# Three small moves in a tuned encoder-decoder kernel: the query weights' sums, a read-out's engine, one block's first token sums

## The chip, the cores and the metric

The kernel runs on one core of a Trainium2 chip. The metric is the device time of one execution in microseconds (us); the median of the runs counts. Five engines work side by side, each through its own queue in order: TensorE (PE in the profile, its weight loads PEld), VectorE (DVE), ScalarE (ACT), GpSimd (POOL) and SyncE (SP), which issues the DMA transfers. They meet by semaphores.

## The reference, cut to what matters

One encoder layer over a short context (2 x 77 rows) and one decoder layer over 2 x 2048 rows, all in float32, width 512, 16 heads of 32, feed-forward width 2048.

```python
memory = encoder_layer(ctx_1024)                     # attention, then relu feed-forward, 77 rows a batch
y = x                                                # (2, 2048, 512)
yn = ln(y, dec_n1)
y = y + mha(yn, yn, dec_sa_in_w, dec_sa_out_w, bias=relative + causal)
y = y + mha(ln(y, dec_n2), memory, dec_ca_in_w, dec_ca_out_w, bias=relative)
y = y + relu(ln(y, dec_n3) @ ff1_w.T + ff1_b) @ ff2_w.T + ff2_b
# inside mha: q = xq @ wq.T + bq; the scores are divided by sqrt(32), the softmax runs over keys
```

## The kernel before, in words

The 2 x 2048 rows are cut into eight blocks (b, m) of 512 rows, numbered x = 0 to 7. For causal self-attention a block has 4 groups g of 4 heads and 4 tiles t of 128 rows, so 16 units a block; unit n has a slot n. The order is written by hand. `light[n]` holds steps run at the start of a slot, `jobs[n]` the projections on TensorE, `late[n]` steps at its end; between slots stand scores (L375, read out by VectorE in L384 and L391, with the negated row maxima at L401), exponentials on ScalarE (L406), transposes on TensorE (L426, copied out at L431 and L433) and the products with the values (L455, copied out by ScalarE at L466 for a batch's first block). Every engine keeps the order in which the code emits.

The projections of blocks 1 to 3 of each batch use a Strassen-like scheme of seven products of quarters. It needs sums of weight quarters, made once by GpSimd and stored in DRAM, and four sums T1 to T4 of token quarters for each block (`token_sums`, L961, from the normalised and transposed rows `nT`). T1 and T2 lie in buffers `xt`, T3 and T4 in `xr`.

- The k, v and output weights' sums are made by `wc_sums` (loads L977, sums L981 and L961, stores `wc_store` L993) in slots 2, 9 and 12, those of the query weights by three steps: `q_load` (8 transfers, L1013), `q_sums` (four scalings L1020, an add L1022, three subtractions L961) and `q_store` (7 transfers, L1029, from where `pair_job` loads them at L1037). All use the same eight spare pieces of `kT`: four take the loaded quarters, four the sums.
- The encoder, a long chain of small stages, runs beside block 0: stage n goes to `late[n]`, or `late[n + 2]` from the tenth on. In slots 6 to 9 GpSimd subtracts the maxima (L617), adds a bias row to the residual (L655) and divides by the sums (L629) for it; VectorE adds the bias and takes the maxima (L615, L616, and sums at L627); ScalarE does the exponentials (L622); TensorE the scores (L606).
- In the same slots block 1's rows are loaded (L275), their statistics taken by VectorE (L282 to L285), a power and the centring done by GpSimd (L286, L293), the transposes by TensorE (L305) and their read-out by ScalarE and VectorE (L310, L312).
- `pair_job` with parts (1, 6) makes two products of a query group pair side by side in one PSUM bank (L1048). The first is read out with its bias at L1054, the second added to that at L1055, by VectorE.
- Block results get their residual on GpSimd at L1106 and L1107 (`out_done`) once the rows have been loaded; the softmax division of a group is one GpSimd product at L493.

After the self-attention of all blocks come cross attention and feed-forward (from about 1500 us on).

Of the kernel before, what the change touches and what calls it, by code (L numbers as in the profile page):

```python
# [10 lines left out]
F32 = mybir.dt.float32  # L11
AF = mybir.ActivationFunctionType
ALU = mybir.AluOpType
# [4 lines left out]
P = 128  # L18
B, T, S, D = 2, 2048, 77, 512
# [5 lines left out]
NMB = T // MB  # L25
# [29 lines left out]
def tile_encoder_decoder(ctx: ExitStack, tc: tile.TileContext, ins, out):  # L55
    nc = tc.nc
    x, src = ins["x"], ins["ctx_1024"]
# [13 lines left out]
    qbias = const.tile([P, NC], F32, name="qbias")  # L71
# [87 lines left out]
    with (  # L159
# [20 lines left out]
        def bank():  # L180

            ring.append(ring.pop(0))
            return psum[:, ring[-1], :]
# [11 lines left out]
        wbig, xs, xr, ots_at = {}, {}, {}, {}  # L195
# [214 lines left out]
        got = {}  # L410
# [547 lines left out]
        gp, ve = nc.gpsimd, nc.vector  # L958

        def minus(engine, out, a, b):  # L960
            engine.tensor_tensor(out, a, b, ALU.subtract)  # L961
# [3 lines left out]
        def sum_n(name, of):  # L965
            minus(gp, of(name), *(of(a) for a in T_OF[name]))
# [42 lines left out]
        def q_load(z):  # L1009
            src = ins["dec_sa_in_wT"][:, :D].rearrange("(c k p) (h r o) -> p c h r k o", c=2, k=2, h=2, r=2)  # L1010
            for i, (r, c) in enumerate(((0, 0), (0, 1), (1, 0), (1, 1))):
                for h in range(2):
                    nc.sync.dma_start(  # L1013
                        z[i][:, ts(h, TOK)].rearrange("p (k o) -> p k o", k=2), src[:, c, h, r]
                    )

        def q_sums(z):
            q = {(0, 0): z[0], (0, 1): z[1], (1, 0): z[2], (1, 1): z[3]}
            for t in z[:4]:
                gp.tensor_scalar(t, t, SCALE, None, ALU.mult)  # L1020
            s1, s2, s3, s4 = z[4:]
            gp.tensor_tensor(s1, q[1, 0], q[1, 1], ALU.add)  # L1022
            minus(gp, s2, s1, q[0, 0])
            minus(gp, s3, q[0, 0], q[1, 0])
            minus(gp, s4, q[0, 1], s2)

        def q_store(z):
            for i, t in enumerate((z[0], z[1], z[3], *z[4:])):
                nc.sync.dma_start(saq_d[i], t)  # L1029

        def pair_job(b, m, h, parts):

            def load():
                w = sb.tile([P, NC, P], F32, name="wqk", tag="wqk", bufs=3)
                for j, i in enumerate(parts):
                    src = saq_d[Q_OPS.index(PARTS[i][0])][:, ts(h, TOK)]
                    nc.sync.dma_start(w[:, 2 * j : 2 * j + 2, :], src.rearrange("p (k o) -> p k o", k=2))  # L1037
                return w

            def run(w):  # L1040
                if parts[0] == 1:
                    for g in (2 * h, 2 * h + 1):
                        qTs[b, m, g] = sb.tile([P, MB], F32, name="q", tag="q", bufs=3)
                mm = bank()
                for j, i in enumerate(parts):
                    n = of_nT(b, m, PARTS[i][1])
                    for c in range(2):
                        nc.tensor.matmul(mm[:, ts(j, TOK)], w[:, 2 * j + c, :], n[:, c, :], start=c == 0, stop=c == 1)  # L1048
                d = {
                    f"{r + 1}{c + 1}": qTs[b, m, 2 * h + r][:, ts(c, TOK)] for r in range(2) for c in range(2)  # L1050
                }
                got = [mm[:, ts(j, TOK)] for j in range(len(parts))]
                if parts == (1, 6):
                    nc.scalar.activation(d["11"], got[0], AF.Identity, bias=qbias[:, 2 * h : 2 * h + 1])  # L1054
                    ve.tensor_tensor(d["12"], got[1], d["11"], ALU.add)  # L1055
                elif parts == (7, 4):
                    ve.scalar_tensor_tensor(d["22"], got[0], qstep[:, h : h + 1], d["12"], ALU.add, ALU.add)
                    ve.tensor_tensor(d["21"], got[1], d["22"], ALU.add)
                elif parts == (2, 5):
                    q = qTs[b, m, 2 * h]  # L1060
                    ve.tensor_tensor(q, mm, q, ALU.add)
                    ve.tensor_tensor(d["22"], got[1], d["22"], ALU.add)
                else:
                    assert parts == (3,)
                    ve.tensor_tensor(d["12"], got[0], d["12"], ALU.add)

            return load, run, True
        n_tiles = {}
        PARTS = {
# [5 lines left out]
        def of_nT(b, m, name):  # L1075
            if name[0] == "T":
                return n_tiles[b, m][int(name[1]) - 1].rearrange("p (c o) -> p c o", c=2)
            r, c = int(name[0]) - 1, int(name[1]) - 1
            return nTs[b, m][:, 2 * r : 2 * r + 2, ts(c, TOK)]

        def token_sums(b, m):
            n_tiles[b, m] = [
                sb.tile([P, D], F32, name=tag, tag=tag, bufs=2) for tag in ("xt", "xt", "xr", "xr")
            ]
            for name in ("T1", "T2", "T3", "T4"):
                sum_n(name, lambda n: of_nT(b, m, n))

        o_tiles = {}
# [92 lines left out]
        light = {n: [] for n in range(-1, len(units) + NU)}  # L1181
        late = {n: [] for n in light}

        for x, (b, m) in enumerate(blocks):
            u = x * NU
# [12 lines left out]
            else:  # L1198
# [7 lines left out]
                for at, names in todo.items():  # L1206
                    for name in names.split():
                        h, parts = "ab".find(name[0]), tuple(int(i) for i in name[1:])
# [29 lines left out]
                    on = nc.vector if x == 1 and t % 2 else nc.scalar  # L1238
                    light[turned_at].append(lambda b=b, m=m, t=t, on=on: norm_turn(b, m, t, on=on))
            if not first:  # L1240
                (late[u - 5] if x == 1 else light[u - 5 if x == NMB + 1 else u - 6]).append(
                    lambda b=b, m=m: token_sums(b, m)
                )
            for g in range(NC):
                apart = not (x == len(blocks) - 1 and g >= NC - 2)
                d = spread(b, m, g) if apart else divide(b, m, g)
# [63 lines left out]
        )  # L1310
        spare = [kT[:, g, (2 + h) * MB : (3 + h) * MB] for g in range(NC) for h in range(2)]
        light[1].append(q_steps)
        light[5].append(lambda: q_load(spare))
        late[6].append(lambda: q_sums(spare))
        late[7].append(lambda: q_store(spare))
        for n, kind in ((2, "k"), (9, "v"), (12, "o")):
            light[n].append(lambda kind=kind: wc_sums(sa_name[kind], True, spare, sa_from[kind]))
            late[n + 1].append(lambda kind=kind: wc_store(sa_d[kind], spare))
# [141 lines left out]
        u = 2 * NU  # L1460
# [5 lines left out]
        u = 6 * NU  # L1466
# [522 lines left out]
```

## Time and profile before

| | |
|---|---|
| median of 3 runs | 2736.42 us (2736.1 to 2736.77) |
| the profiled execution | 2739.72 us, its span in the trace 2737.9 us |
| busy share of the span | PE 99%, PEld 81%, DVE 67%, ACT 56%, POOL 37% |
| POOL, 98 to 130 us | 31.44 of 32 us |
| PE, 98 to 130 us | 24.64 of 32 us, granted clock 0.84 |

The span runs from the first to the last instruction of the profiled execution. Times in a timeline are microseconds from the span's start; a row merges neighbours of one kind, and its bracket names the idle time of the engine just before it and what ended it. The granted clock is the share of TensorE's full clock in that stretch.

### The profile page before, as it was taken

To read this page: it belongs to the slowest core of one execution; us is meant where nothing else is said; L and a number is where in the kernel's file an instruction comes from. 1 tells how busy PE (TensorE), PEld (TensorE's weight loads), DVE (VectorE), ACT (ScalarE), POOL (GpSimd) and SP (SyncE) were. 2 spreads that over 40 slices of the span, in tenths; PEclk is the share of its full clock that TensorE was granted. 3 is DMA by queue.
4 is the path that set the end of the run, shared out by engine and by line. 5 is a ranking of instruction groups with operands and counts; after the bars stand their busy time and mean duration, and the time that the engine had idled before them with its cause. 6 is when DMAs were issued, how large, how long until landed. Compare 5 with 4: busy or idle time off the path is not lost.

```text
span 2737.9 us, 68226 instructions
## 1 busy us (share of the span) xinstructions
PE 2710.3 (99%) x26606; PEld 2216.0 (81%) x26606; DVE 1836.3 (67%) x5390; ACT 1540.5 (56%) x3006; POOL 1002.5 (37%) x844
## 2 busy tenths in 40 slices
PE   9899999999999999999999999999999999999998
PEld 5578877777876677777777877898989898989898
DVE  5676588888876577688788793646464746464645
ACT  3445557767787546767767785444444444444431
POOL 1702226500210512313300103465646564646456
PEclk9999999999999999999999999999999999999999
DMA  8634446511212531342411106575758575756575
GB/s 224 194 108 130 137 142 180 164 56 48 63 48 72 143 91 59 113 142 80 138 56 35 61 20 228 166 219 166 218 167 242 166 219 166 220 166 219 149 225 185
DMA packets 296276, 385.10 MB, mean 141 GB/s; under 512 B 41184, under 2 KB 165648, under 8 KB 295826
## 3 DMA queue, kind: packets, MB, share of 16 engines
q1 hardware_dynamic: 295954, 380.73, 46.1%
q8 instruction: 211, 3.46, 0.5%
q14 instruction: 111, 0.91, 0.1%
HBM read 334.15 MB, written 46.47 MB: 139 GB/s over the span
## 4 chain that ended last, share of the span: by engine, by line
PE 94%; DVE 2%; ACT 1%; POOL 1%; issue 1%; DMA 0%; SPq 0%; DVEq 0%; POOLq 0%; ACTq 0%
PE psum L426 18%; PE psum L1633 14%; PE psum L1662 12%; PE psum L375 11%; PE psum L455 9%; PE psum L1136 8%; PE psum L1796 3%; PE psum L1753 3%; PE psum L1048 2%; PE psum L865 2%; PE psum L835 1%; PE psum L873 1%; PE psum L589 1%; PE psum L239 1%; PE psum L810 1%; PE psum L226 1%
## 5 line engine op out<-in xcount | busy, mean ns | idle before, releaser
L406 ACT ACTIVATE pp<-pp,nm 128x128 f32<-128x128 f32 (+15 forms) x512 | 612.1, 1201 | 29.3 <-DVE nm L401 28.7
L384 DVE TENSOR_SCALAR_CACHE_REDUCE pp<-psum 128x512 f32<-128x512 f32 (+3 forms) x1024 | 556.2, 591 | 53.2 <-PE psum L375 50.7
L433 ACT COPY pts<-psum 128x512 f32<-128x512 f32 (+2 forms) x730 | 382.5, 580 | 309.6 <-PE psum L426 260.9
L426 PE MATMUL psum<-ident,pp 128*128 128x128 f32 x4352 | 531.3, 277 | 4.9 <-ACT nT L310 2.4
L426 PEld LDWEIGHTS psum<-ident,pp 128*128 128x128 f32 x4352 | 472.6, 141 | 57.6 <-DVE pp L384 21.7
L375 PE MATMUL psum<-kT,q 32*128 32x512 f32 (+3 forms) x2560 | 335.0, 559 | 8.1 <-ACT oT L466 4.2
L455 PEld LDWEIGHTS psum<-pts,vv 128*32 128x32 f32 x8704 | 225.6, 110 | 127.8 <-DVE pp L384 55.4
L1662 PE MATMUL psum<-pp 128*128 128x128 f32 x2560 | 304.5, 276 | 1.9 <-POOL pp L961 1.6
L431 DVE COPY pts<-psum 128x512 f32<-128x512 f32 (+3 forms) x406 | 252.5, 654 | 78.5 <-PE psum L426 76.4
L1662 PEld LDWEIGHTS psum<-pp 128*128 128x128 f32 x2560 | 296.3, 192 | 8.6 <-issue 2.8
L455 PE MATMUL psum<-pts,vv 128*32 128x128 f32 x8704 | 278.7, 275 | 0.7 <-DVE mx L391 0.3
L961 POOL TENSOR_TENSOR pp<-pp 128x512 f32<-128x512 f32 x159 | 212.8, 1355 | 112.8 <-DMA pp<-in_dec_ff_wT_dram 51.7
L1633 PE MATMUL psum<-vv,pp 128*128 128x256 f32 x1024 | 236.2, 381 | 0.0
L375 PEld LDWEIGHTS psum<-kT,q 32*128 32x128 f32 x2560 | 145.7, 183 | 111.5 <-issue 39.9
L1633 PEld LDWEIGHTS psum<-vv,pp 128*128 128x128 f32 x1024 | 190.3, 190 | 25.8 <-issue 0.5
L391 DVE CUSTOM_DVE_ANT_0 pp<-psum,bias 128x256 f32<-128x256 f32 (+1 forms) x512 | 196.0, 411 | 20.0 <-PE psum L375 19.8
L1646 DVE TENSOR_TENSOR kT<-kT,psum 128x512 f32<-128x512 f32 x96 | 65.8, 686 | 191.3 <-PE psum L1633 191.1
L1649 ACT ACTIVATE kT<-kT,vecs 128x256 f32<-128x256 f32 x192 | 87.1, 502 | 157.2 <-DVE kT L1646 156.6
L1633 PE MATMUL psum<-nT,pp 128*128 128x256 f32 x768 | 174.1, 380 | 0.0
L1633 PEld LDWEIGHTS psum<-nT,pp 128*128 128x128 f32 x768 | 144.2, 190 | 20.3 <-issue 1.6
L1670 ACT COPY oT<-psum 128x128 f32<-128x128 f32 x56 | 15.0, 268 | 238.9 <-PE psum L1662 238.9
L493 POOL TENSOR_TENSOR oT<-rirows,oT 128x512 f32<-128x512 f32 x30 | 38.4, 1281 | 290.0 <-DMA rirows<-rec 223.7
(274 smaller groups left out, 4110.7 us busy)
## 6 DMA issues: line engine op xcount, KB each, us to landing
pp<-w_d SPq DMA_DIRECT2D x520, 256.0 KB
pp<-in_dec_ff_wT_dram SPq DMA_DIRECT2D x112, 256.0 KB
bias<-tzg SPq DMA_DIRECT2D x128, 128.0 KB
pp<-wo_d SPq DMA_DIRECT2D x56, 256.0 KB
wqk<-in_dec_sa_in_wT_dram SPq DMA_DIRECT2D x52, 256.0 KB
wqk<-sa_q SPq DMA_DIRECT2D x84, 128.0 KB
vv<-in_enc_ff_wT_dram SPq DMA_DIRECT2D x8, 1024.0 KB
xr<-in_x_dram SPq DMA_DIRECT2D x32, 256.0 KB
```

The costliest lines, as they stand in the source:

```text
L375: nc.tensor.matmul(banks[r][:, : kn * P], q[rows4(r), ts(t, P)], kT[rows4(r), g, k0 * P : (k0 + kn) * P], start=True, stop=True,)
L384: nc.vector.tensor_scalar(p[:, k0 : k0 + far], s[:, :far], 1.0, None, ALU.mult, ALU.max, accum_out=st["mx"][:, r, c : c + 1],)
L391: nc.vector.tensor_tensor_reduce(p[:, k0 + far : i + 1], s[:, far:kn], near[:, 2 - (kn - far) :], 1.0, LOWEST, ALU.add, ALU.max, accum_out ...
L406: nc.scalar.activation(p, p, AF.Exp, bias=nm, accum_out=to)
L426: nc.tensor.transpose(pt[:, ts(x, P)], state[n]["p"][r][:, k], ident)
L431: nc.vector.tensor_copy(pts[:, : len(load), :], pt[:, :w])
L433: nc.scalar.copy(pts[:, : len(load), :], pt[:, :w])
L455: nc.tensor.matmul(ot[rows4(r)], vv[:, k, ts(g * HC + r, HD)], got.pop((n, k, r)), start=k == k0 and (whole or not begun), stop=k == k1 - ...
L961: engine.tensor_tensor(out, a, b, ALU.subtract)
L1136: nc.tensor.matmul(mm[:, ts(f, TOK)], left[:, c, ts(f, P)], right[:, c, :], start=c == 0, stop=c == 1,)
L1633: nc.tensor.matmul(mm[:, ts(f, TOK)], a[:, c, ts(f, P)], b[:, c, :], start=fresh and f == 0 and c == 0, stop=c == 1, skip_group_check=True,)
L1662: nc.tensor.matmul(psum[:, bank_i, ts(col, P)], lhs[:, c, :], w[:, c, :], start=fresh and k in (0, 3) and c == 0, stop=c == 3, skip_group_ ...
```

## The change

Three edits. The query weights' loads go from the start of slot 5 to the start of slot 4, their sums from the end of slot 6 to the end of slot 4, their stores from the end of slot 7 to the end of slot 6. The first product of each pair is read out by VectorE instead of ScalarE (12 places). Of the sixth block (x = 5) the sums T1 and T2 are made at the start of slot 74 instead of 75, in a function that now makes two sums a call; T3 and T4 stay.

```diff
                 if parts == (1, 6):
-                    nc.scalar.activation(d["11"], got[0], AF.Identity, bias=qbias[:, 2 * h : 2 * h + 1])
+                    ve.tensor_scalar(d["11"], got[0], qbias[:, 2 * h : 2 * h + 1], None, ALU.add)
                     ve.tensor_tensor(d["12"], got[1], d["11"], ALU.add)
...
-        def token_sums(b, m):
-            n_tiles[b, m] = [
-                sb.tile([P, D], F32, name=tag, tag=tag, bufs=2) for tag in ("xt", "xt", "xr", "xr")
-            ]
-            for name in ("T1", "T2", "T3", "T4"):
+        def token_sums(b, m, tag):
+            n_tiles.setdefault((b, m), []).extend(sb.tile([P, D], F32, name=tag, tag=tag, bufs=2) for _ in range(2))
+            for name in ("T1", "T2") if tag == "xt" else ("T3", "T4"):
                 sum_n(name, lambda n: of_nT(b, m, n))
...
-                (late[u - 5] if x == 1 else light[u - 5 if x == NMB + 1 else u - 6]).append(
-                    lambda b=b, m=m: token_sums(b, m)
-                )
+                for tag in ("xt", "xr"):
+                    (late[u - 5] if x == 1 else light[u - 5 if x == NMB + 1 and tag == "xr" else u - 6]).append(
+                        lambda b=b, m=m, tag=tag: token_sums(b, m, tag)
+                    )
...
-        light[5].append(lambda: q_load(spare))
-        late[6].append(lambda: q_sums(spare))
-        late[7].append(lambda: q_store(spare))
+        light[4].append(lambda: q_load(spare))
+        late[4].append(lambda: q_sums(spare))
+        late[6].append(lambda: q_store(spare))
```

GpSimd's queue in block 0, the difference between before (-) and after (+): L1020, L1022 and the three L961 behind them are `q_sums`; L286 and L293 are the power and the centring of block 1's first tile, L617 and L655 the encoder's.

```order
 L961 TENSOR_TENSOR kT<-kT 128x512 x3
-L286 TENSOR_TENSOR rstd<-rstd,mhalf 128x1
-L293 TENSOR_SCALAR xt<-xt,bnmv,rstd 128x512
-L617 TENSOR_TENSOR pp<-pp,emx 77x1232
-L655 TENSOR_TENSOR pp<-pp 77x512 x2
 L1020 TENSOR_SCALAR kT<-kT 128x512 x4
 L1022 TENSOR_TENSOR kT<-kT 128x512
 L961 TENSOR_TENSOR kT<-kT 128x512 x3
+L286 TENSOR_TENSOR rstd<-rstd,mhalf 128x1
+L293 TENSOR_SCALAR xt<-xt,bnmv,rstd 128x512
+L617 TENSOR_TENSOR pp<-pp,emx 77x1232
+L655 TENSOR_TENSOR pp<-pp 77x512 x2
```

The eight operations of `q_sums` now stand directly behind the key weights' sums and ahead of five operations that used to precede them.

SyncE's queue, first where the query weights' loads (L1013) now stand, and then where the stores (L1029) do: L993 stores the key weights' sums, L199 loads a slice of projection weights, L544 an encoder weight, L94 writes a bias table and L275 loads rows of block 1.

```order
 L544 DMA vv<-in_enc_out_wT_dram 128x4x512
 L993 DMA sa_k<-kT 128x512 x4
+L1013 DMA kT<-in_dec_sa_in_wT_dram 128x2x128 x8
 L199 DMA wqk<-in_dec_sa_in_wT_dram 128x4x128
 L544 DMA vv<-in_enc_ff_wT_dram 128x4x512
```

```order
 L94 DMA tz_72<-pp 16x32x384
+L1029 DMA sa_q<-kT 128x512 x7
 L275 DMA xr<-in_x_dram 128x512
 L199 DMA wqk<-in_dec_sa_in_wT_dram 128x4x128
-L1029 DMA sa_q<-kT 128x512 x7
 L275 DMA xr<-in_x_dram 128x512
```

The loads moved up past the loads and stores of one slot, and the stores past one row load and one weight load.

GpSimd's queue ahead of the sixth block, before: the last three `out_done` pairs of an earlier block, a softmax division, then the four token sums (`xt` are T1 and T2, `xr` are T3 and T4).

```order
L1107 TENSOR_TENSOR xr<-xr,wbig 128x512
L1106 TENSOR_TENSOR xr<-xr,row_dec_sa_out_b 128x512
L1107 TENSOR_TENSOR xr<-xr,wbig 128x512
L1106 TENSOR_TENSOR xr<-xr,row_dec_sa_out_b 128x512
L1107 TENSOR_TENSOR xr<-xr,wbig 128x512
L493 TENSOR_TENSOR oT<-rirows,oT 128x512
L961 TENSOR_TENSOR xt<-nT 128x512
L961 TENSOR_TENSOR xt<-nT,xt 128x512
L961 TENSOR_TENSOR xr<-nT 128x512
```

And the same place of the changed kernel, where L1104 and L1105 are the lines that were L1106 and L1107:

```order
L1105 TENSOR_TENSOR xr<-xr,wbig 128x512
L961 TENSOR_TENSOR xt<-nT 128x512
L961 TENSOR_TENSOR xt<-nT,xt 128x512
L1104 TENSOR_TENSOR xr<-xr,row_dec_sa_out_b 128x512
L1105 TENSOR_TENSOR xr<-xr,wbig 128x512
L1104 TENSOR_TENSOR xr<-xr,row_dec_sa_out_b 128x512
L1105 TENSOR_TENSOR xr<-xr,wbig 128x512
L493 TENSOR_TENSOR oT<-rirows,oT 128x512
L961 TENSOR_TENSOR xr<-nT 128x512
```

T1 and T2 went ahead of two pairs and the division.

## The prediction

> **What bounds the kernel now.** I read the page first: its busy times, then the PE's list of waits, then windows, the chain and the timelines where the waits lie.
>
> ```profile
> PE 2710.3 (99%) x26606; PEld 2216.0 (81%) x26606; DVE 1836.3 (67%) x5390; ACT 1540.5 (56%) x3006; POOL 1002.5 (37%) x844
> ...
> PE psum L375 <- ACT oT L466: 4.2, 1, 4.2
> PE psum L426 <- ACT nT L310: 2.4, 2, 2.0
> ...
> 60.00:82.00 22.00, 21.72 (x178) 11.83 (x176) 12.49 (x46) 7.98 (x26) 3.02 (x3) 1.00 0.78 213
> 82.00:98.00 16.00, 14.18 (x142) 8.13 (x142) 12.66 (x43) 7.73 (x21) 13.21 (x10) 1.00 0.70 190
> 98.00:130.00 32.00, 24.64 (x157) 17.01 (x156) 17.80 (x78) 18.26 (x54) 31.44 (x24) 0.84 0.60 190
> 130.00:200.00 70.00, 69.66 (x644) 50.87 (x643) 54.58 (x193) 30.78 (x74) 8.74 (x8) 1.00 0.40 121
> ```
>
> TensorE is busy for 2710.3 of 2737.9 us, so only its 27.6 us of idle time, and time at a lowered clock, can be won or lost quickly. The second part of the fence is the list of PE's waits (total, times, longest); the third is windows (length, then busy us of PE, PEld, DVE, ACT and POOL, granted clock, DMA share, GB/s). Between 98 and 130 us PE idles 32 - 24.64 = 7.4 us and runs at 0.84 of its clock, while POOL is busy for 31.44 of 32 us. In the window before 82 us POOL did 3.02 us of work in 22; from 130 us on PE has no gap of weight. The chain of work that ended last tells who held PE:
>
> ```profile
> 88.97 5.89 POOL kT L1020 x4
> ...
> 101.90 2.06 POOL xt L293
> 103.96 2.22 POOL pp L617
> 106.21 0.03 ACT pp L622
> ...
> 107.34 0.57 ACT oT L466
> ...
> 107.96 1.80 PE psum L375 x4
> ...
> 120.91 1.40 ACT nT L310 x4
> ...
> 122.35 1.95 PE psum L426 x12
> 124.30 2.99 PE psum L1136 x8
> ...
> 129.02 1.73 PE psum L1136 x8
> ```
>
> Read from the top: the query weights' sums hold GpSimd from 88.97 us, behind them come block 1's centring and the encoder's second subtraction L617, ScalarE's exponential L622 waits for that, the copy L466 stands behind it in ScalarE's queue, and the scores L375 on PE wait for the bank that L466 empties. This is not GpSimd's whole load but its order.
>
> **Part 1: the query weights' sums, two slots sooner.** These are GpSimd's rows and SyncE's around the old and the new place:
>
> ```profile
> 51.57 3.74 POOL L961 TENSOR_TENSOR kT<-kT 128x512 f32<-128x512 f32 x3
> 76.92 0.55 POOL L286 TENSOR_TENSOR rstd<-rstd,mhalf 128x1 f32<-128x1 f32 x1 [21.61 <-DVE rstd L285]
> ...
> 81.61 2.25 POOL L617 TENSOR_TENSOR pp<-pp,emx 77x1232 f32<-77x1232 f32 x1 [1.95 <-DVE emx L616]
> ...
> 99.97 1.27 POOL L493 TENSOR_TENSOR oT<-rirows,oT 128x512 f32<-128x512 f32 x1
> ...
> 37.71 8.23 SPq L977 DMA_DIRECT2D kT<-in_dec_sa_in_wT_dram  x4
> ...
> 55.71 0.50 SPq L199 DMA_DIRECT2D wqk<-in_dec_sa_in_wT_dram  x1
> 62.71 0.38 SPq L544 DMA_DIRECT2D vv<-in_enc_ff_wT_dram  x1
> ...
> 71.54 4.32 SPq L1013 DMA_DIRECT2D kT<-in_dec_sa_in_wT_dram  x8
> ```
>
> The eight operations took 99.97 - 88.97 = 11.0 us, the last thing behind which everything to 130 us queued. Their new place is GpSimd's idle stretch of 21.6 us from 55.3 to 76.92. SyncE has a gap there too, from 56.2 to 62.71, so the eight loads (4.32 us of issue) go out from about 55.7 to 60, perhaps 61 since earlier transfers are still in flight. How long they fly the trace of before doesn't show, as GpSimd came to them late; the nearest row is the key weights' load, last issued before 45.94, on which GpSimd worked from one operation (1.25 us) ahead of the L961 of 51.57, so from 50.3: 4.4 us from the end of issue. Taken again, the last load is there at about 65; one scaling (1.5) and four sums (5.0) follow, so GpSimd is free at 72, 5 us ahead of L286. The moved loads pass L199, L544 and the transfers between; no row in the list of PE's waits names a transfer, so a few microseconds of delay there stay hidden. The transfers behind the old place (71.54) go up to 4.3 us sooner. The stores L1029 no longer wait for late sums on SyncE, with the row load L275 of block 1's last tile behind them.
>
> What is late next. Without the 11.0 us ahead of it ScalarE's L622 runs near 95 instead of 106.21, and the 4.2 us wait of L375 is gone. But VectorE is next, and its rows say how far PE may move:
>
> ```profile
> 86.51 0.79 PE L606 MATMUL psum<-pp 32*77 32x77 f32 x32
> ...
> 87.62 0.69 DVE L282 BATCH_NORM_STATS2 bnst<-xt 128x6 f32<-128x512 f32 x1 [2.29 <-DMA xt<-in_x_dram]
> 88.64 1.62 DVE L615 TENSOR_TENSOR pp<-psum,pp 77x308 f32<-77x308 f32 x4
> ...
> 103.15 0.70 DVE L282 BATCH_NORM_STATS2 bnst<-xr 128x6 f32<-128x512 f32 x1 [2.75 <-DMA xr<-in_x_dram]
> ...
> 109.11 0.22 DVE L384 TENSOR_SCALAR_CACHE_REDUCE pp<-psum 128x128 f32<-128x128 f32 x1
> ...
> 112.29 0.42 DVE L431 COPY pts<-psum 128x256 f32<-128x256 f32 x1 [0.41 <-PE psum L426]
> 113.63 1.37 DVE L312 TENSOR_SCALAR nT<-psum,vecs 128x128 f32<-128x128 f32 x4 [0.91 <-PE psum L305]
> ...
> 102.81 0.91 PE L375 MATMUL psum<-kT,q 32*128 32x384 f32 x4
> ```
>
> From 109.11 to the L310 of 120.91 VectorE works with only two gaps, 0.41 and 0.91, both waiting for a PE on a lowered clock; at its end come that L310 and the L426 of 122.35. PE's first scores of this unit began at 102.81, so VectorE could have begun at about 103.2 (an estimate: the first head's product later) had it not waited for the load of the row of 103.15 and for the sums of the late exponentials: it can begin 109.11 - 103.2 = 5.9 us sooner. The two gaps of 1.3 us mostly close at full clock. And the wait of 2.29 us for block 1's second tile, whose load stood behind L1013, goes: L615 then starts when TensorE's L606 is done, at 86.51 + 0.79 = 87.3 instead of 88.64, 1.3 us. Together 5.9 + 1.3 + 1.3 = 8.5 us at 122.35, and after 130 us PE is bound by itself, so this carries to the end. The wait of 2 us before that L426 stays, as it is made by VectorE's and ScalarE's own work there. Bounds: at least the 4.2 us wait itself; at most all idle time and lowered clock from 82 to 130 us, 1.8 + 7.4 + 0.16 x 32 = 14.3 us. I take 8.5, the row-by-row sum.
>
> One rule on the clock: behind the 4.2 us wait the trace shows four matmuls of L375 in 1.80 us, against 0.91 for as many at 102.81, and behind the last wait of only 2 us L1136 took 2.99 us against 1.73 a little later, so 1.3 us of lowered clock stays in the sum. The Trainium skill (TensorE: Matmul & The Clock Gate, What's actually happening) puts the lowered clock after an idle window of about 3.4 us; by it the 2 us wait alone would not lower the clock and the sum would be 9.8, so the traces differ from the rule unless the earlier waits had a share.
>
> **Part 2: the read-out on VectorE.** One place shows its worth, at 1038 us; the last line is from the view of L1055, what its engine waited for in total.
>
> ```profile
> 1037.93 0.47 ACT L1054 ACTIVATE q<-psum,qbias 128x256 f32<-128x256 f32 x1
> 1038.43 0.42 DVE L1055 TENSOR_TENSOR q<-psum,q 128x256 f32<-128x256 f32 x1 [3.05 <-ACT q L1054]
> 1038.91 0.91 PE L375 MATMUL psum<-kT,q 32*128 32x384 f32 x2 [1.04 <-DVE q L1055]
> ...
>   ACT q L1054: 23.1, 11
> ```
>
> ScalarE's read-out stood behind exponentials while VectorE idled 3.05 us, and PE waited 1.04 us for the bank. On VectorE the pair runs when the products are done, within those 3.05 us: gain 1.0 us. VectorE's form of the operation isn't in the trace; its neighbour L1055 takes 0.42 for the same shape from PSUM, so 12 x 0.42 = 5.1 us more VectorE work. It is covered: VectorE idled ahead of 11 of the 12 places, 23.1 us in all, waiting for just this operation. If that cover failed everywhere the price would be the 5.1 us; I take 0.
>
> **Part 3: T1 and T2 of the sixth block.**
>
> ```profile
> 950.08 1.27 POOL L1106 TENSOR_TENSOR xr<-xr,row_dec_sa_out_b 128x512 f32<-128x512 f32 x1 [7.17 <-DMA xr<-in_x_dram]
> ...
> 956.48 1.51 POOL L961 TENSOR_TENSOR xt<-nT 128x512 f32<-128x512 f32 x1
> ...
> 959.51 1.13 PE L1048 MATMUL psum<-xt,wqk 128*128 128x256 f32 x4 [1.49 <-POOL xt L961]
> ```
>
> GpSimd idles 7.17 us ahead of 950.08 and the two sums (1.5 us each) fit in it; the two pairs behind them wait for rows that land at 950 anyway. PE's 1.49 us wait goes. T3 and T4 then follow L493 3 us sooner. Gain 1.5.
>
> **Sum.** 8.5 + 1.0 + 1.5 = 11.0 us off the profiled execution's span of 2737.9, so 2726.9. That execution took 2739.72 in all, 3.3 above the median of the runs shown, 2736.42; the difference carries over: 2725.4.
>
> **Rivals.** (a) Something else holds PE between 98 and 130 us, the norm read-outs L310 and L312 or a late transfer, and only the 4.2 us wait goes: 4.2 + 2.5 = 6.7, 2729.7. For it: VectorE's dense stretch; against: that stretch starts late for a reason that goes. (b) All idle time and lowered clock goes, 14.3 + 2.5: 2719.6. Against: the last 2 us wait is VectorE's. (c) The clock stays up behind the 2 us wait, 1.3 us more gain: 2724.1; the page on the clock named above would have it so; the row of 2.99 us speaks against. (d) Part 1 doesn't do what it says, since L622 is then held by another link (rows for L655, statistics): 2.5 us, 2733.9. (e) Slower: GpSimd works in order, and L286, L293, L617 and L655 now stand behind an operation that waits for eight loads. It costs nothing while the last load lands by 70.4 (76.92 less 6.5); L617 waited 1.95 us for VectorE, so the encoder's chain, and with it PE, feels it from 72.4 on, a microsecond each. A landing at 85 would undo part 1's gain and add 12.6: 2736.4 - 2.5 + 12.6 = 2746.5. Against: it needs 24 us of flight, where the key weights' took 4.4.
>
> **How the numbers follow.** Chances: forecast 0.54, (a) 0.16, (b) 0.08, (c) 0.10, (d) 0.08, (e) 0.04. The measurement of this kernel tells about 0.2% (5.5 us) from no change. The forecast, (b), (c) and most of (a), which sits close to the edge at 6.7, are faster by more: 0.85. (d) and 3 in 100 of (a) are the same: 0.11. (e) is slower: 0.04. The range from 2719.5 to 2730.5 reaches from (b) to just past (a) and leaves out (d), (e) and the tails.
>
> **What would show it.** In the changed profile: L1020 between 60 and 68 us and no idle PE ahead of the L375 near 102; POOL below 70% in 98 to 130; L310's wait at L426 still there near 114; no wait of PE for `xt` near 950 and none for L1055 near 1030; VectorE's L1054 at 0.42. Wrong would be an L1020 that starts after 70, an L622 for the second batch still after 100, or new waits of PE on VectorE at the twelve places.

## The result, and the profile after

Nine runs of the changed kernel took 2730.39 us in the median (2728.05 to 2733.07), nine of the kernel before 2736.77 (2735.73 to 2741.35). The medians are 6.4 us apart; the ratio on record for these runs is 0.9973, 95% interval [0.9963, 0.9983], so 7.4 us less, with 4.7 to 10.1 in the interval. The comparison was made once more on another occasion (the experiment after_again below): 0.9965 [0.9952, 0.9977], 9.6 us less. The forecast was 11.0 us less, above the first interval and inside the second, and a range of 6 to 17. The median of 2730.39 lies 0.1 us inside the slow end of that range, 2730.5. The profiled execution has a span of 2726.9 us, the span that the sum gave; it took 2728.76 in all. That the span agrees to the tenth is luck, as the steps below show: one term came out smaller, one mostly vanished, and a chance effect of the clock made up for both. The profile of before is of an execution 3.0 us above its median, and that of the changed kernel of one 1.6 us below; the prediction had carried the first of these over as a constant.

The page of the changed kernel, first part, and then two rows of PE's list of waits (total, times, longest):

```profile
PE 2707.0 (99%) x26606; PEld 2214.9 (81%) x26606; DVE 1842.0 (68%) x5402; ACT 1534.6 (56%) x2994; POOL 1000.8 (37%) x844
```

```profile
PE psum L426 <- ACT nT L310: 3.2, 2, 1.8
...
PE psum L426 <- DVE kT L1147: 0.3, 1, 0.3
```

The 4.2 us wait for L466's bank is out of the list. L310's row stayed and grew from 2.4 to 3.2. The windows view (length, busy us of PE, PEld, DVE, ACT and POOL, clock, DMA share, GB/s) of the changed kernel, the last row for the same 32 us as before:

```profile
60.00:82.00 22.00, 21.43 (x175) 11.33 (x173) 13.31 (x52) 8.05 (x26) 14.70 (x11) 1.00 0.97 251
82.00:98.00 16.00, 14.52 (x142) 8.17 (x143) 13.88 (x50) 9.50 (x25) 13.67 (x10) 1.00 0.84 235
...
98.00:130.00 32.00, 28.78 (x287) 21.27 (x285) 23.61 (x93) 18.92 (x60) 21.82 (x17) 1.00 0.64 201
```

GpSimd took 11.7 us of work forward into the 22 us where it had idled (14.70 busy instead of 3.02), and from 98 to 130 us it is busy for 21.82 instead of 31.44. PE is busy 4.1 us longer in that stretch and at the full clock, which was 0.84. The timeline of GpSimd shows the step itself:

```profile
61.27 5.88 POOL L1020 TENSOR_SCALAR kT<-kT 128x512 f32<-128x512 f32 x4 [7.01 <-DMA kT<-in_dec_sa_in_wT_dram]
67.23 1.26 POOL L1022 TENSOR_TENSOR kT<-kT 128x512 f32<-128x512 f32 x1
68.58 3.71 POOL L961 TENSOR_TENSOR kT<-kT 128x512 f32<-128x512 f32 x3
76.11 0.57 POOL L286 TENSOR_TENSOR rstd<-rstd,mhalf 128x1 f32<-128x1 f32 x1 [3.82 <-DVE rstd L285]
...
89.70 2.25 POOL L617 TENSOR_TENSOR pp<-pp,emx 77x1232 f32<-77x1232 f32 x1 [0.27 <-DVE emx L616]
```

The sums wait 7.01 us for their loads, begin at 61.27 and end at 72.3; GpSimd then idles 3.82 us ahead of L286. The second subtraction L617 runs at 89.70 instead of 103.96, when its input is there, not when the queue lets it. ScalarE and VectorE, in their timelines, follow:

```profile
92.30 1.21 ACT L622 ACTIVATE pp<-pp 77x1232 f32<-77x1232 f32 x1
95.69 0.58 ACT L466 COPY oT<-psum 128x512 f32<-128x512 f32 x1 [2.18 <-PE psum L455]
```

```profile
101.64 0.29 DVE L384 TENSOR_SCALAR_CACHE_REDUCE pp<-psum 128x128 f32<-128x128 f32 x1 [0.73 <-PE psum L375]
```

L466 now waits for PE, where PE waited for it, and VectorE's first maxima begin at 101.64 instead of 109.11. PE's timeline over the same place:

```profile
100.70 0.93 PE L375 MATMUL psum<-kT,q 32*128 32x384 f32 x8
...
108.13 1.20 PE L426 MATMUL psum<-ident,pp 128*128 128x128 f32 x9 [1.41 <-ACT nT L310]
...
113.83 1.53 PE L426 MATMUL psum<-ident,pp 128*128 128x128 f32 x12 [1.81 <-ACT nT L310]
115.19 1.89 PE L1134 MATMUL psum<-nT,wqk 128*128 128x256 f32 x8
```

Two waits for the norm's read-out are left, and behind the second one the clock stays up: the product of eight took 2.99 us before (there it was L1136) and takes 1.89.

The two programs issue the same 26606 matmuls in the same order, so the start of any one of them can be compared across traces. This table gives, for every kernel run, the start minus that of the same matmul in the trace of before; 113.83 - 122.35 is the -8.52 of its first row. The first column lies ahead of every edit: it differs by up to 1.4 us from the trace of before, and is taken off where a term is read. A term is the difference of two columns. The columns 122.35 and 131.79 of e2 and e3 lie ahead of the edits of these two kernels, so they show how far executions of the same instructions differ there: 0.75 and 3.09 us, with the first column taken off.

| at, us of before | 13.54 | 122.35 | 131.79 | 956.57 | 959.51 | 968.01 | 1036.52 | 1038.91 |
|---|---|---|---|---|---|---|---|---|
| after | -0.80 | -8.52 | -10.21 | -10.20 | -11.85 | -10.18 | -10.68 | -11.91 |
| after_again | -0.80 | -8.36 | -10.04 | -10.02 | -11.67 | -10.59 | -9.60 | -10.83 |
| after_third | -1.23 | -8.96 | -10.64 | -10.63 | -12.28 | -11.04 | -10.04 | -11.27 |
| e1_query_sums | -0.54 | -8.20 | -8.21 | -8.19 | -8.80 | -8.73 | -8.51 | -8.51 |
| e2_readout | -0.33 | -1.08 | -1.09 | -1.08 | -1.61 | -1.02 | -0.99 | -2.22 |
| e3_token_sums | 0.39 | -2.70 | -2.71 | -2.70 | -4.35 | -3.95 | -4.61 | -4.61 |
| e4_shorter | -0.25 | -4.88 | -4.89 | -4.86 | -4.73 | -4.74 | -4.34 | -4.35 |
| e5_memset | 0.19 | -7.53 | -7.54 | -7.50 | -9.15 | -8.62 | -8.85 | -10.08 |
| e6_scalar_sixth | -1.05 | -8.42 | -10.10 | -10.10 | -11.75 | -11.11 | -11.39 | -12.62 |
| e7_best | -0.08 | -7.15 | -8.84 | -8.83 | -10.48 | -8.53 | -9.18 | -10.41 |
| e8_parts12 | -1.16 | -8.59 | -8.60 | -8.56 | -8.99 | -8.40 | -8.08 | -9.31 |
| e9_split | -1.42 | -6.03 | -6.98 | -6.97 | -8.62 | -8.25 | -8.90 | -10.13 |

### The profile page after: what moved, and what is told of

The parts are those of the page before. It is cut to its first block, busy times and chain, and to the rows that moved or that the text cites. A ratio compares the mean times of both kernels' runs of the same rounds, so it can differ in the third digit from the quotient of the medians.

```text
span 2726.9 us, 68245 instructions
## 1 busy us (share of the span) xinstructions
PE 2707.0 (99%) x26606; PEld 2214.9 (81%) x26606; DVE 1842.0 (68%) x5402; ACT 1534.6 (56%) x2994; POOL 1000.8 (37%) x844
## 4 chain that ended last, share of the span: by engine, by line
PE 95%; DVE 2%; ACT 1%; issue 1%; POOL 1%; DMA 1%; SPq 0%; POOLq 0%; DVEq 0%; ACTq 0%
PE psum L426 18%; PE psum L1632 14%; PE psum L1661 13%; PE psum L375 11%; PE psum L455 9%; PE psum L1134 8%; PE psum L1795 3%; PE psum L1752 3%; PE psum L1048 3%; PE psum L865 2%; PE psum L835 1%; PE psum L873 1%; PE psum L589 1%; PE psum L810 1%; PE psum L239 1%; PE psum L215 1%
## 5 line engine op out<-in xcount | busy, mean ns | idle before, releaser
L426 PE MATMUL psum<-ident,pp 128*128 128x128 f32 x4352 | 530.5, 276 | 5.9 <-ACT nT L310 3.2
L426 PEld LDWEIGHTS psum<-ident,pp 128*128 128x128 f32 x4352 | 472.1, 141 | 58.9 <-DVE pp L384 21.6
L375 PE MATMUL psum<-kT,q 32*128 32x512 f32 (+3 forms) x2560 | 332.9, 559 | 2.1 <-ACT nT L310 0.7
L961 POOL TENSOR_TENSOR pp<-pp 128x512 f32<-128x512 f32 x159 | 212.7, 1354 | 112.2 <-DMA pp<-in_dec_ff_wT_dram 51.5
L375 PEld LDWEIGHTS psum<-kT,q 32*128 32x128 f32 x2560 | 145.0, 183 | 104.7 <-issue 38.5
```

What stands on the lines that cost most here:

```text
L375: nc.tensor.matmul(banks[r][:, : kn * P], q[rows4(r), ts(t, P)], kT[rows4(r), g, k0 * P : (k0 + kn) * P], start=True, stop=True,)
L426: nc.tensor.transpose(pt[:, ts(x, P)], state[n]["p"][r][:, k], ident)
```

## The experiments

**Part 1 alone.** The kernel before with this edit:

```
-        light[5].append(lambda: q_load(spare))
-        late[6].append(lambda: q_sums(spare))
-        late[7].append(lambda: q_store(spare))
+        light[4].append(lambda: q_load(spare))
+        late[4].append(lambda: q_sums(spare))
+        late[6].append(lambda: q_store(spare))
```

> Only the query weights' loads, sums and stores are moved; the read-out and the sixth block's sums stay as before. Theory (GpSimd's order in block 0 was the stall): nearly the whole gain is here, 8 to 10 us in the trace at block 1's first products and in the span, a ratio of about 0.9965; L375 has no wait for L466. Rival (the gain is the sum of three like parts, or the profiled run was a lucky one): 3 us or less, ratio 0.999.

Measured: 2731.7 us, ratio 0.9977 [0.9968, 0.9986], span 2729.4. At 122.35 PE stands 8.20 - 0.54 = 7.66 us sooner, as in the changed kernel (8.52 - 0.80 = 7.72). Behind it the two part, in PE's timeline:

```profile
114.15 2.68 PE L426 MATMUL psum<-ident,pp 128*128 128x128 f32 x12 [1.81 <-ACT nT L310]
116.62 2.46 PE L1136 MATMUL psum<-nT,wqk 128*128 128x256 f32 x8
```

The same wait of 1.81 us stands here, and the clock does go down behind it. Part 1 is most of the gain: 6.3 us by the ratio, far above the rival's 3, though less than the 8 to 10 us and the 0.9965 that the theory named. What the clock does behind the last wait isn't set by the edit.

**Part 2 alone.** The kernel before with this edit:

```
-                    nc.scalar.activation(d["11"], got[0], AF.Identity, bias=qbias[:, 2 * h : 2 * h + 1])
+                    ve.tensor_scalar(d["11"], got[0], qbias[:, 2 * h : 2 * h + 1], None, ALU.add)
```

> Only the pair's first product is read out by VectorE. Theory: PE's wait of 1.0 us for L1055 near 1038 us goes and nothing else changes: 1.0 to 1.5 us less, ratio 0.9995. Rival (VectorE's 12 x 0.45 us lie on PE's path): up to 5 us more, ratio 1.002.

Measured: 2736.26 us, ratio 0.9991 [0.9982, 1.0]. VectorE's timeline at the one place:

```profile
1035.69 0.48 DVE L1054 TENSOR_SCALAR q<-psum,qbias 128x256 f32<-128x256 f32 x1 [1.30 <-PE psum L1048]
1036.21 0.42 DVE L1055 TENSOR_TENSOR q<-psum,q 128x256 f32<-128x256 f32 x1
```

VectorE now waits 1.30 us for PE's product, no longer 3.05 for ScalarE, and PE has no wait there: 2.22 - 0.99 = 1.23 us won. All nine traces with part 2 show this 1.23 and the three without it 0, so this term is settled although the total, at the upper end of whose interval no change still lies, can hardly tell it.

**Part 3 alone.** The kernel before with this edit:

```
-            if not first:
-                (late[u - 5] if x == 1 else light[u - 5 if x == NMB + 1 else u - 6]).append(
...
+                for tag in ("xt", "xr"):
+                    (late[u - 5] if x == 1 else light[u - 5 if x == NMB + 1 and tag == "xr" else u - 6]).append(
```

> Only T1 and T2 of the sixth block are made a slot sooner; the read-out stays on ScalarE. Theory (the wait goes, but T3 and T4 then run beside VectorE's L845, which takes longer and hands PE a later start): the 1.5 us wait of L1048 goes and about 0.7 us comes back within 10 us of it, net 0.5 to 1.0 us less. Rival (the giveback in the changed kernel came from VectorE's extra read-out alone): the full 1.5 us stays and L845 takes 0.55 us as before.

Measured: 2737.95 us, ratio 0.9998 [0.9989, 1.0007]. At 959.51 PE is 4.35 - 2.70 = 1.65 us sooner, and 1.25 of it is left at 968, between the theory's 0.5 to 1.0 and the rival's 1.5. In the profiled execution it was lost again at 1035 and 1062, where the clock went down for 3.4 and 6.8 us. The changed kernel won the same 1.65 and had given back all of it by 968, so the question was what gives it back. VectorE's timeline of the changed kernel, and behind it GpSimd's, show the suspect:

```profile
946.11 1.34 DVE L845 TENSOR_TENSOR pp<-pp,cmx 128x308 f32<-128x308 f32 x1
...
948.38 0.75 DVE L845 TENSOR_TENSOR pp<-pp,cmx 128x308 f32<-128x308 f32 x1
...
951.88 0.48 DVE L1054 TENSOR_SCALAR q<-psum,qbias 128x256 f32<-128x256 f32 x1
...
952.73 0.68 DVE L1147 TENSOR_TENSOR kT<-psum,kT 128x512 f32<-128x512 f32 x1
```

```profile
945.84 1.27 POOL L961 TENSOR_TENSOR xr<-nT 128x512 f32<-128x512 f32 x1
947.53 1.27 POOL L961 TENSOR_TENSOR xr<-nT,xt 128x512 f32<-128x512 f32 x1 [0.42 <-DMA y<-xr]
```

The first L845 begins 0.27 us after a sum of GpSimd and takes 1.34 us, as if it began when the sum was done. In the kernel with part 3 alone the order was the other way, L845 0.26 us ahead of the sum, and the sum took longer:

```profile
953.60 0.65 DVE L845 TENSOR_TENSOR pp<-pp,cmx 128x308 f32<-128x308 f32 x1
```

```profile
953.86 1.52 POOL L961 TENSOR_TENSOR xr<-nT 128x512 f32<-128x512 f32 x1
```

**A shorter sum at the old place.** The kernel before without the four scalings L1020:

```
-            for t in z[:4]:
-                gp.tensor_scalar(t, t, SCALE, None, ALU.mult)
```

> The kernel before, with the four scalings of the query weights (L1020, 5.9 us) left out and everything in its old place. Theory (the length of GpSimd's queue ahead of the encoder's L617 is the stall): L617 and L622 of the second batch come 5.9 us sooner, the wait of L375 for L466 falls below 1 us, and 5 to 6 us are gained at block 1's first products. Rival (SyncE's loads and stores around the sums are the stall): the wait stays above 3 us and the gain is below 2 us.

Measured: 2733.97 us, ratio 0.9979 [0.9969, 0.9988]. ScalarE's timeline of this kernel:

```profile
100.28 1.23 ACT L622 ACTIVATE pp<-pp 77x1232 f32<-77x1232 f32 x1 [4.86 <-POOL pp L617]
101.42 0.56 ACT L466 COPY oT<-psum 128x512 f32<-128x512 f32 x1
```

With 5.9 us less in GpSimd's queue, and nothing moved, L622 runs 106.21 - 100.28 = 5.9 us sooner, and L466 behind it; at 122.35 PE has 4.88 - 0.25 = 4.6 of it. PE's wait of 4.2 us for L466 is out of its list. The length of the queue ahead of L617 held PE, since loads and SyncE's order were left as they were. It isn't the whole of part 1: L655, right ahead of these sums, waited 2.96 us for a transfer in this execution, and part 1 lets that transfer out sooner (see the part on why).

**The sixth block without T3 and T4.** The changed kernel, those two tiles zeroed, their sums left out:

```
+                if tag == "xr" and (b, m) == (1, 1):
+                    gp.memset(n_tiles[b, m][int(name[1]) - 1], 0.0)
+                    continue
```

> The changed kernel, with T3 and T4 of the sixth block filled by zeros on GpSimd instead of summed (those two sums are left out). Theory, that GpSimd's sums and VectorE's L845 share the access to SBUF and what PE won there was lost through VectorE: L845 near 946 to 951 us takes 0.48 to 0.6 us each time instead of 1.34 and 0.75, TensorE no longer waits 0.27 us for kT L1147, and of the 1.6 us that PE won at L1048 xt at least 1 us is still there 5 us later. Rival, that L845 was long for another reason (a transfer, or VectorE alone): one L845 of over 1 us stays, and PE's 0.27 us wait too. In time: 1 to 2 us at most against the changed kernel, inside the scatter.

Measured: 2729.28 us, ratio 0.9965 [0.9952, 0.9979]. VectorE's timeline:

```profile
948.80 0.48 DVE L845 TENSOR_TENSOR pp<-pp,cmx 128x308 f32<-128x308 f32 x1
...
950.21 0.48 DVE L845 TENSOR_TENSOR pp<-pp,cmx 128x308 f32<-128x308 f32 x1
```

All four are at 0.48, PE's wait for L1147 is out of its list, and 8.62 - 7.50 = 1.1 us of part 3 is still there at 968. So GpSimd's sums beside L845 have to do with what was given back. The zeros also take GpSimd less time, 0.5 us each instead of 1.3 to 1.5; but in none of the traces with part 3 does PE wait for T3 or T4 in this stretch, which leaves the overlap.

**The sixth block's read-out on ScalarE again.** The changed kernel with:

```
+                    if (b, m, h) == (1, 1, 0):
+                        nc.scalar.activation(d["11"], got[0], AF.Identity, bias=qbias[:, 2 * h : 2 * h + 1])
+                    else:
```

> The changed kernel, with the read-out L1054 of the sixth block's first pair back on ScalarE, at this one place of the twelve. Theory, that VectorE's extra 0.48 us is part of what the sixth block gave back: L1147 ends 0.3 to 0.5 us sooner after L845, PE's 0.27 us wait for kT L1147 is gone, and PE keeps about 0.5 us more 5 us after L1048 xt. Rival, that only the sums on GpSimd matter: the wait of 0.27 us stays as it was. Time against the kernel before: 0.9970 to 0.9975, as the changed kernel's 0.9973; half a microsecond can't be told in it.

Measured: 2730.37 us, ratio 0.997 [0.9959, 0.9982]. The four L845 took 0.77, 0.53, 0.77 and 0.48, the wait for L1147 is gone, and 1.01 us of part 3 is kept. The two further executions of the changed kernel, with the read-out on VectorE and L845 about as long in total (2.47 and 2.64 us, 2.55 here), kept 0.57 and 0.41. So the read-out may take half a microsecond of part 3 too, as the theory had it; three executions don't settle it.

**And block 0's third key projection read out on VectorE.** The same, with:

```
-                if m >= 2:
+                if m >= 2 or (b, m, g) == (0, 0, 2):
```

> As the one before, and the key projection's read-out L231 of block 0's third group on VectorE instead of ScalarE, where it stood behind four exponentials and PE waited 0.69 us for it near 87 us. Theory: that wait is gone and PE is 0.5 to 0.7 us sooner at the L375 behind it; at 124 us, where VectorE ends the wait, 0 to 0.7 is left, so 2728 to 2731 us and a ratio of 0.9966 to 0.9975. Rival: VectorE, with 0.7 us more ahead of its own scores, hands the same wait on to the L426 of 88.4, and nothing is left at 95 us.

Measured: 2729.33 us, ratio 0.9964 [0.9952, 0.9976]. PE's wait of 0.7 us for L231 is gone from its list, but at 122.35 PE stands 7.15 - 0.08 = 7.07 us sooner, where the kernel without this edit has 7.4: the idle time moved. L845 took 1.35 and 1.55 us here, with the read-out on ScalarE, and all of part 3 was given back: the read-out isn't all that it hangs on. The ratio is the lowest of all, but its interval holds the changed kernel's.

**Parts 1 and 2 without part 3.** The changed kernel with T1 and T2 back at the old place:

```
-                    (late[u - 5] if x == 1 else light[u - 5 if x == NMB + 1 and tag == "xr" else u - 6]).append(
+                    (late[u - 5] if x == 1 else light[u - 5 if x == NMB + 1 else u - 6]).append(
```

> The changed kernel without its third part: T1 and T2 of the sixth block again where they were, parts 1 and 2 kept. Theory, that part 3 was won and given back within 5 us in the changed kernel: PE waits 1.4 to 1.7 us for xt L961 near 948 us again, VectorE's L845 there takes 0.5 to 0.6, and 10 us later PE stands as in the changed kernel within 0.5 us; ratio 0.9970 to 0.9976. Rival, that part 3 keeps its 1.5 us and the profile of the changed kernel shows bad luck in that one execution: PE is 1 to 1.5 us later than in the changed kernel, ratio 0.9977 to 0.9980.

Measured: 2732.16 us, ratio 0.9974 [0.9964, 0.9984]. PE waits 1.06 us for xt L961, less than expected, and from 956.57 to 968 it loses 0.16 us where the changed kernel's three executions win 0 to 0.6. Part 3 is worth about half a microsecond there on average, and the time can't tell it. The theory missed on L845, in VectorE's timeline:

```profile
947.74 1.60 DVE L845 TENSOR_TENSOR pp<-pp,cmx 128x308 f32<-128x308 f32 x1
```

It took 1.60 us, not 0.5 to 0.6, with the sums at their old place: GpSimd's T1 began at 947.74 as well. In e1 and e2 it took 1.42 and 1.50. So moving the sums isn't what makes them meet L845.

**The changed kernel, twice more.** Nothing edited. In every trace so far the stretches at half clock began whole multiples of 3.41 us apart; the question was whether their place decides what the clock does behind the wait near 114 us.

> The changed kernel unaltered, another execution. Theory: the clock is granted over equal windows of 3.41 us whose boundaries lie elsewhere against the kernel in each execution (the starts of the lowered stretches within every trace so far lie whole multiples of 3.41 us apart), and a window in which PE works less than half of the time is followed by one at half clock. If the 1.81 us wait ahead of the L426 near 114 us lies inside one window (a granted clock drop that starts 0.1 to 1.6 us after the wait's end in the time pattern of this trace), L1134 behind it takes 2.4 us or more for eight; if a boundary cuts the wait, it stays at 1.9. Rival: the kernel alone decides; then L1134 takes 1.9 again, as in the first trace of this kernel. Median 2729 to 2732, ratio 0.9965 to 0.998.

> The changed kernel once more, for a third place of the clock's windows against the kernel. Theory as before: the place of the lowered stretches against the kernel differs again, by parts of 3.41 us, and the 2 us around L1134 near 115 us follow from whether the 1.81 us wait lies inside one window. Rival: L1134 takes 1.9 us for eight as in the first trace.

Measured: 2728.54 us, ratio 0.9965 [0.9952, 0.9977], and 2727.68 for the one run of the other. The clock's windows did lie elsewhere, but the rule failed. Where a boundary cuts the wait, in the first trace of the changed kernel and in e6, the clock stayed up, as the theory has it. In both further executions the whole wait lies inside one window, and the clock stayed up all the same. First two windows of the kernel with parts 1 and 2 alone, then two of after_again, each pair cut where the clock of that trace can change:

```profile
111.14:114.55 3.41, 1.60 (x20) 1.21 (x12) 1.50 (x12) 3.04 (x9) 1.58 (x3) 1.00 0.76 242
114.55:117.96 3.41, 3.41 (x13) 2.97 (x12) 1.66 (x4) 2.13 (x9) 3.41 (x3) 0.50 0.02 9
```

```profile
111.61:115.02 3.41, 1.59 (x13) 1.36 (x14) 1.49 (x11) 2.81 (x9) 1.95 (x3) 1.00 0.88 272
115.02:118.43 3.41, 3.41 (x20) 3.05 (x19) 1.42 (x4) 3.01 (x11) 3.41 (x4) 1.00 0.05 11
```

In both the whole wait lies inside one window, and PE works 1.60 and 1.59 of 3.41 us in it; the next window has half the clock in the one and all of it in the other. One difference is how much of L426 behind the wait falls into the window: 0.8 us in the first pair, 1.0 in the second. PE's busy share alone doesn't set it, and what does wasn't found.

**The norm's read-out split between two engines.** The kernel with the sixth block's read-out on ScalarE, and:

```
-                if on is nc.scalar and (c or not apart):
+                if on is nc.scalar and (c or not apart) and not ((b, m) == (0, 1) and c >= 2):
```

> As the kernel with the sixth block's read-out on ScalarE, and in block 1 the norm's two read-outs L310 of 1.47 us are split: two of the four 128x128 stay on ScalarE, two go to VectorE's L312. Theory, that after part 1 these read-outs and the exponentials ahead of them on ScalarE hold PE: the waits of PE's L426 for nT L310, 1.41 and 1.81 us, shrink to 0.6 to 1.2 each, PE stands 0.7 to 1.4 us sooner at 124 us, and the second wait no longer brings a lowered clock behind it, worth another 1.4 us in the executions that had it. Ratio 0.9955 to 0.997. Rival, that VectorE is as full there: its scores' maxima L391 come 0.7 us later twice, ScalarE's exponentials wait for them, and PE stands at 124 us where it stood, within 0.3 us; ratio 0.997.

Measured: 2733.46 us, ratio 0.9979 [0.997, 0.9988], against 0.997 of the kernel that it was made from, with intervals that overlap. VectorE's timeline:

```profile
106.80 2.00 DVE L312 TENSOR_SCALAR nT<-psum,vecs 128x128 f32<-128x128 f32 x6 [2.60 <-ACT nT L310]
108.72 0.41 DVE L384 TENSOR_SCALAR_CACHE_REDUCE pp<-psum 128x256 f32<-128x256 f32 x1
```

Neither theory: here VectorE doesn't read its half of the bank until ScalarE is done with the other (whether by the program's ordering or otherwise wasn't tried), so in its queue it stands 2.60 us, with the next unit's maxima behind it, and 2.76 us at the second place. PE loses 2.8 us at 122.35 (4.61 instead of 7.37 sooner). That L310 behind ScalarE's exponentials holds PE there is seen in the waits; how much a shorter L310 would bring wasn't found.

## Why the prediction was right, and where not

**Part 1, 8.5 us: the mechanism held, the size was 7.4 to 7.7 against the trace of before, and less against others.** In the seven traces that have it and no other edit ahead of this place (the changed kernel three times, e1, e5, e6 and e8; e7 moved one read-out and shows 7.1) PE stands 7.4 to 7.7 us sooner at 122.35 than in the trace of before. The steps: loads there at about 65, measured 61.27 for the first scaling, with the last not in its way; GpSimd free at 72, measured 72.3, though as 61.27 + 11.0 and not as a last load and 6.5; L622 near 95, measured 92.30; L310's wait still there at 114, measured 113.83. VectorE's maxima begin 7.47 us sooner, 6.7 without the shift at the start, against 5.9 + 1.3 in the sum: PE's first scores did come 1.3 sooner, but the maxima follow them by 0.9 us and not by the estimated 0.4. The two gaps gave 1.1 instead of 1.3.

What the sum took for fixed is where the kernel before stands. The kernels with part 2 or part 3 alone run the same instructions up to here, and yet PE stands 0.75 and 3.09 us sooner in them at 122.35. Against them part 1 is worth about 6.9 and 4.5 us. The sums stand behind L655, which adds a row to the encoder's residual once transfers have landed. GpSimd's timelines of before, of part 2 alone and of part 3 alone:

```profile
86.39 2.49 POOL L655 TENSOR_TENSOR pp<-pp 77x512 f32<-77x512 f32 x2 [2.54 <-DMA pp<-in_rows_dram]
```

```profile
85.33 2.49 POOL L655 TENSOR_TENSOR pp<-pp 77x512 f32<-77x512 f32 x2 [1.81 <-DMA rirows<-rec]
```

```profile
84.23 2.50 POOL L655 TENSOR_TENSOR pp<-pp 77x512 f32<-77x512 f32 x2
```

With the shift at the start taken off, L622 comes 0.76 and 2.56 us sooner in the last two than in the first. VectorE has the like at block 1's second tile, for which it waited 2.29 us in the trace of before. Its timelines of the kernel with part 2 alone, and then of the one with part 3 alone:

```profile
86.59 0.69 DVE L282 BATCH_NORM_STATS2 bnst<-xt 128x6 f32<-128x512 f32 x1 [1.59 <-DMA xt<-in_x_dram]
87.61 1.62 DVE L615 TENSOR_TENSOR pp<-psum,pp 77x308 f32<-77x308 f32 x4
```

```profile
87.70 1.63 DVE L615 TENSOR_TENSOR pp<-psum,pp 77x308 f32<-77x308 f32 x4 [0.76 <-PE psum L606]
```

Both waits are there in three of the four traces without part 1 (e4 has 2.96 and 2.72 us) and in none of the nine with it: the loads L1013 no longer stand ahead of the two transfers, and SyncE issues them 3 to 4 us sooner. So part 1 takes these waits away, as the prediction had it for the second; what that brings depends on how late the transfers would have been, and four traces don't say what is usual.

**Part 2, 1.0 us: 1.23.** L1054 takes 0.48 us on VectorE, not 0.42, and the cover held at all twelve places: VectorE waits 11.4 us for the products ahead of 11 L1054, none of them for anything else, and PE's list has no row for either operation (PE's weight loads wait for L1055 three times, 1.3 us in all, where it was 2.4).

**Part 3, 1.5 us: won (1.65) and mostly given back, the step that failed.** The prediction priced the moved sums on GpSimd and left out what VectorE runs beside GpSimd there. In the seven traces with part 3 and its sums, PE still has 0.6 us of the 1.65 at 968 on average, and on the whole the less, the longer the four L845 are in total:

| | e9 | e3 | after_again | e6 | after_third | after | e7 |
|---|---|---|---|---|---|---|---|
| four L845, us | 2.29 | 2.30 | 2.47 | 2.55 | 2.64 | 3.05 | 3.86 |
| left at 968, us | 1.28 | 1.25 | 0.57 | 1.01 | 0.41 | -0.02 | -0.30 |

With the tiles zeroed the four take 1.92 and 1.1 us is left. (The block's read-out L1054 is on ScalarE in e3, e6, e7 and e9.) The waits that PE's list shows there mostly name VectorE, L842 ahead of an L845 or L1147 behind the last, with at most 0.3 us each; the rest of the loss stands as longer matmuls, in the changed kernel 1.34 us for eight L375 instead of 0.71. L845 can be as long with the sums at the old place (1.42, 1.50 and 1.60 for the first one in e1, e2 and e8, 0.56 in the trace of before); but there PE waits for T1 and T2 anyway, and only with that wait gone does VectorE's delay reach it. That last step is read from the waits and wasn't tried by itself.

**The clock, rival (c).** I kept 1.3 us of lowered clock behind the 2 us wait. In three of three profiles of the changed kernel it stayed up, worth 10.21 - 8.52 = 1.7 us, as rival (c) had it and as the Trainium skill (TensorE: Matmul & The Clock Gate, What's actually happening) would have it for a wait shorter than its window. But behind the same wait of 1.81 us the clock went down in e1, e4, e5 and e8. Both ends were possible, and neither the row nor the rule alone decides.

So the sum by the runs, against the trace of before: 7.6 + 1.2 + 0 to 0.6 for part 3, 0 to 1.7 for the clock: 8.8 to 11.1. Less the 1.3 us by which the three executions of the old order stand ahead of that trace on average (0, 0.75 and 3.09), it is 7.5 to 9.8, an estimate from three; the two comparisons gave 7.4 and 9.6. The profiled pair shows 11.0 because the execution after started 0.8 us ahead and had the clock's 1.7; it also lost 0.9 us later (11.91 sooner at 1038.91, 11.02 at the matmul of 2639), the net of 1.6 us behind a lowered clock near 1114 us and of smaller gains.

**The others.** (e), late loads, is excluded with 3.8 us to spare at L286, and (d) by L622 at 92.30. (a), only the 4.2 us wait and so 6.7 us in all, isn't excluded by the time, since the first interval holds 6.7. In the traces PE is 7.4 to 7.7 us further at 122.35, more than 4.2, but against the execution of part 3 alone only 4.5; and the read-outs L310 that (a) names do hold PE now, for 3.2 us. (b) would have needed the waits of 1.41 and 1.81 us at L426 to go; they are there in every trace with part 1 that leaves the read-outs of block 0 and block 1 as they are. No run beats the changed kernel by more than the intervals allow.

## What to carry to other kernels

Where an engine is 37% busy and yet holds the others up, look at the order of its queue: moving eight operations into its idle stretch, with their loads, brought most of the gain, and a queue shortened by 5.9 us at the old place brought 4.6. When a step moves and a wait goes, ask what the other engines run beside it and which of them ends the next wait, not only whether the step's own engine is free. A term that hangs on one transfer or on the clock in one execution is a chance: here unchanged instructions stood up to 3.1 us apart in two traces of the same stretch, so a second trace of the kernel before is worth taking before anything is added up.

## What the runs showed of the hardware

A two-operand operation of GpSimd and one of VectorE, both on SBUF operands, hold each other up where they overlap, and the later one pays: L845, 0.48 us alone, took 1.34 us when it began 0.27 us after GpSimd's sum of 1.27. The Trainium skill (SBUF — State Buffer, SBUF: two separate sides) has the two engines share a port pair that the one that starts first holds for its whole instruction. The rows agree to 0.15 us: 1.27 - 0.27 of waiting and 0.48 of work are 1.48, measured 1.34. In the kernel with part 3 alone GpSimd's division comes first:

```profile
952.63 1.29 POOL L493 TENSOR_TENSOR oT<-rirows,oT 128x512 f32<-128x512 f32 x1
```

It ends at 953.92, so L845, which began at 953.60, has 0.32 of waiting and 0.48 of work, 0.80, measured 0.65. L845 ends at 954.25, so the sum that began at 953.86 has 0.39 and 1.27, 1.66, measured 1.52.

The clock goes down without a long idle time, and at places that move. Between the program's start and its end the half-clock stretches of every trace are 3.41 us or two of them long and begin on a grid of 3.41 us, whose place against the kernel differs from execution to execution. Some follow a window in which PE had hardly a gap; this is the changed kernel near 1114 us, by windows and then by PE's timeline:

```profile
1110.41:1113.83 3.42, 3.37 (x28) 1.12 (x28) 3.42 (x15) 3.42 (x7) 2.59 (x3) 0.99 0.22 83
1113.83:1117.24 3.41, 3.41 (x45) 3.02 (x37) 1.95 (x13) 1.16 (x4) 3.33 (x3) 0.51 0.21 80
```

```profile
1109.17 4.20 PE L375 MATMUL psum<-kT,q 32*128 32x512 f32 x16
1113.30 2.39 PE L455 MATMUL psum<-pts,vv 128*32 128x128 f32 x48
1115.62 3.58 PE L426 MATMUL psum<-ident,pp 128*128 128x128 f32 x24
```

The window ahead is full of score products that use 32 of the 128 rows. The Trainium skill (TensorE: Matmul & The Clock Gate, What's actually happening) has windows of 3.41 us that run free of the kernel, which agrees, and an idle window as what lowers the clock, which doesn't: here the window ahead was busy for 3.37 us, and for 1.60 in the kernel with parts 1 and 2. That products on few rows count as little activity would explain these places; it wasn't tried. With PE's busy time weighted by the share of the 128 rows in use, every one of the 33 drops in the thirteen traces follows a window at about 0.47 or below; but some 110 other windows lie below that and weren't followed by one. Each such stretch costs about 1.6 us near 1114 us, and they come and go between executions. That they are a good part of why runs of one kernel lie several microseconds apart is likely and not shown: of the ten runs without the scalings, the two at a mean granted clock of 0.999 took 2730.1 us and the one at 0.996 took 2737.5.
